# New ranks in a planned eight-layer transformer kernel, with an earlier start: what they do to the time

## The chip, the cores and the metric

The kernel runs on one core of one Trainium2 chip. The metric is device microseconds of one execution; the time before is the median of three runs. Engines are named as the profile names them: PE (TensorE matmul), PEld (TensorE weight load), DVE (VectorE), ACT (ScalarE), POOL (GpSimd) and SP (SyncE, which here only issues transfers).

## The reference

The input x has 8 sequences of 256 tokens of width 128, in fp32. Eight residual blocks follow one another, each with a layer norm ahead of it (`x = x + f(layernorm(x))`):

1. causal attention with one head: scores from `w_q` and `w_k` (width 64), softmax over the keys so far, values through `w_v1` and then `w_v2`;
2. a feed-forward block of width 512 with relu (only the first of eight experts counts, as the router's weights are set to one for it), with a layer norm of its own on input plus result;
3. attention without softmax, (theta phi^T) g over the sequence, so that it can be done as products of 128x128 matrices;
4. the same feed-forward block again;
5. retention with 16 heads: rotated queries and keys, a decaying causal mask, a norm for each head, a silu gate;
6. a feed-forward block of width 384, silu(gate) times up, with integer weights;
7. softmax attention with 16 heads of width 8, and low-rank additions to its weights;
8. the silu feed-forward block again.

Sequences are independent of each other through all of it.

## The kernel before

**Tiling.** The 8 sequences are 4 groups of two; a group's activations are one tile `x[g]` of 128 partitions by 4 token tiles by 128 columns. A matmul over a whole group gives a 128x512 result, one PSUM bank of fp32. There are 8 banks, and small pools of SBUF buffers (`work`, `small`, `probs`, `wide`, and others).

**Order.** Nothing in the code fixes the order of instructions by hand. While the program is built, a planner (`Plan`) runs all groups and layers as Python threads (generators). A thread yields what it needs next: `step(engine, us)`, an engine for an estimated time; `get(store)`, a buffer or a bank; `join`, other threads; `until`, a condition. The planner keeps a clock for each engine, goes through the steps in the order of its estimated times, and sends the thread on, which then issues its real instructions. Where several steps could start on an engine at once, the one of the thread with the lowest `rank` goes first (line 240), and after that the older one. Stores give out their items by rank too (`Store.next`). The order that results is written into each engine's queue and stays fixed; engines run their queues in that order and wait on semaphores. `HANDOFF`, `LOAD`, `NEW_MODE` and `LEEWAY` are costs that the planner adds to its estimates and no instructions.

**Ranks.** `plan.start(thread, rank, us)` starts a thread at a time. Before, group g runs all eight layers at rank g (`layers`), so group 0 always goes ahead of group 1, and so on. Preparing the weights (`causal_weights`, `linear_weights`, `retention_weights`, `silu_weights`, `softmax_weights`), filling the constant buffers (`constants`) and the very last feed-forward of each group have rank `LAST`, 4. The thread that forms the score matrices of the softmax attention, `pairs_of_scores`, has rank `FIRST`, -1.

**Start.** The inputs are loaded at the head of the program, x of group 0 in two halves. `causal_weights` multiplies the weights of the first layer with each other (lines 421 and 422) and copies the products from PSUM to SBUF (lines 424 and 425). `normalised` does a layer norm: for each tile, statistics on VectorE (lines 488 and 489), then four small operations for the whole group on GpSimd (lines 491 to 494: epsilon, sign, power, product), then the normalising on ScalarE or VectorE (lines 500 and 505). `transposed` transposes on TensorE (line 520) and copies to SBUF (line 393). `causal_attention` then waits for the products, and its first matmuls are the values (`by_tiles`, line 548) and the queries (line 561).

**Middle.** `ffn_relu` goes up at line 680 (activation at line 683) and down at line 693. `retention` has many matmuls on parts of the array (lines 816, 874, 896 and 904).

**Score stage.** In `softmax_attention_and_ffn` each sequence has 16 heads, taken two at a time: 8 items for the maxima (`firsts`) and 8 for the exponentials (`seconds`). `pairs_of_scores` puts one item (8 matmul instructions of line 1092, two banks) or two items side by side in the array's rows (16 instructions, four banks) on TensorE. After it come the maxima on VectorE (line 1113) or the exponentials on ScalarE (line 1147), and later the weighted sum (line 1164). Until the last group has been projected it holds four banks and waits to place two items at once. Then `todo["alone"]` is set, it takes two banks more, and two items go together only where two further banks are free at that moment; otherwise one goes by itself. The last feed-forward (lines 1006, 1012 and 1022) works on half a group at a time.

Of the kernel before, what the change touches and what calls it, by code (L numbers as in the profile page):

```python
# [33 lines left out]
P = 128  # L34
# [29 lines left out]
TABLE_LOAD = 1.3  # L64
NEW_MODE = 0.09
LOAD = 0.1
LEEWAY = 0.2


def of_act(n):  # L70
# [50 lines left out]
class Plan:  # L121
# [19 lines left out]
    def spawn(self, steps, rank=None):  # L141

        c = self.current
        th = Thread(steps, c.rank if rank is None else rank, c.t if c else 0.0, c.last if c else None)
        self.resume(th, None)
        return th
# [8 lines left out]
    def put(self, store, *items, later=0.0):  # L155
        for item in items:
            self.count += 1
            store.items.append((self.current.after() + later, self.count, item))
# [37 lines left out]
    def run(self):  # L196
        self.go = []
        while True:
            while self.go:
                self.resume(self.go.pop(0), None)  # L200
            fired = [u for u in self.untils if u[1]()]
            if fired:
                u = fired[0]
                self.untils.remove(u)
                u[0].t, u[0].last = max(u[0].after(), self.now), None
                self.resume(u[0], None)
                continue
            best = None
            if self.sleeping:
                best = (min(self.sleeping)[0], None, None)  # L210
            for e, queue in self.steps.items():
                if queue:
                    start = max(self.free[e], min(q[0] for q in queue))
                    if best is None or start < best[0]:
                        best = (start, e, None)
            for s in self.stores:
                found = s.next()
                if found and (best is None or found[0] < best[0]):
                    best = (found[0], None, s)
            if best is None:  # L220
                break
            start, e, s = best
            self.now = max(self.now, start)
            if e is None and s is None:
                nap = min(self.sleeping)
                self.sleeping.remove(nap)
                nap[2].t, nap[2].last = max(nap[2].t, start), None
                self.resume(nap[2], None)
                continue
            if s is not None:  # L230
                w = s.next()[1]
                s.waiting.remove(w)
                found = s.chosen(w[2])
                s.items = [i for i in s.items if not any(i is f for f in found)]
                got = [i[2] for i in found]
                w[0].t, w[0].last = start, None
                self.resume(w[0], got[0] if w[2] == 1 else got)
                continue
            able = [q for q in self.steps[e] if q[0] <= start]
            q = min(able, key=lambda q: (q[4] not in (None, self.table), q[1].rank, q[2]))  # L240
            _, th, _, us, table = q
            for queue in self.steps.values():
                queue[:] = [r for r in queue if r[1] is not th]
            if table not in (None, self.table):
                us += TABLE_LOAD
                self.table = table
            if e == PE:
                if th.mode != self.mode:
                    us += NEW_MODE
                elif q[0] > self.free[e] - LOAD:  # L250
                    us += LOAD
                self.mode = th.mode
            th.t, th.last = start + us, e
            self.free[e] = th.t
            self.resume(th, e)
        stuck = [s.waiting for s in self.stores if s.waiting] + self.untils
        assert not stuck, f"the plan is stuck at {self.now}: {stuck}"


def step(engine, us, table=None, mode=None):  # L260
    return ("step", ((engine, us, table),), mode)
# [6 lines left out]
def get(store, n=1):  # L268
    return ("get", store, n)


def join(threads):
    return ("join", list(threads))
# [11 lines left out]
def hybrid(ctx: ExitStack, tc: tile.TileContext, t: dict, out: bass.AP):  # L285
    nc = tc.nc
    plan = Plan()
    put, spawn = plan.put, plan.spawn
    FIRST, LAST = -1, GROUPS

    const = ctx.enter_context(tc.tile_pool(name="const", bufs=1))
    psum = ctx.enter_context(tc.tile_pool(name="psum", bufs=1, space=bass.MemoryType.PSUM))
# [66 lines left out]
    banks = [psum.tile([P, N], F32, tag=f"bank{i}", name=f"bank{i}") for i in range(8)]  # L359
    bank = plan.store(banks, strict=True)  # L360

    score_bank = plan.store([])
    work = buffers("work", 28, [P, WORK])
    small = buffers("small", 16, [P, P])
# [51 lines left out]
    def causal_weights():  # L416

        w = buffer("a_w", [P, 2, P])
        ps = yield get(bank)
        yield step(PE, 0.9)  # L420
        nc.tensor.matmul(ps[:, :P], a_t[:, 0, :], a_t[:, 1, :], start=True, stop=True)
        nc.tensor.matmul(ps[:, P : 2 * P], a_t[:, 2, :], a_v2, start=True, stop=True)
        yield step(DVE, 0.4)
        nc.vector.tensor_scalar_mul(w[:, 0, :], ps[:, :P], 0.125)
        nc.vector.tensor_copy(w[:, 1, :], ps[:, P : 2 * P])
        put(bank, ps)
        made["causal"] = w

    def linear_weights():

        w = buffer("b_w", [P, P])
        ps = yield get(bank)
        yield step(PE, 0.25)
        nc.tensor.matmul(ps[:, :P], b_tp[:, 1, :], b_tp[:, 0, :], start=True, stop=True)
        yield step(DVE, 0.2)
        nc.vector.tensor_scalar_mul(w, ps[:, :P], float(D**-0.5))
        put(bank, ps)
        made["linear"] = w
# [38 lines left out]
        made["softmax"] = w  # L477


    def layernorm(src, y):  # L480
        s = yield get(small)
        nt = src.shape[1]
        stats = view(s, "p (t c) -> p t c", 6 * nt, t=nt)
        mv = s[:, 24 : 24 + 2 * nt].rearrange("p (t c) -> p t c", t=nt)
        rstd, shift = s[:, 32 : 32 + nt], s[:, 36 : 36 + nt]
        for i in range(nt):
            yield step(DVE, 0.4)
            nc.vector.bn_stats(stats[:, i, :], src[:, i, :])  # L488
            nc.vector.bn_aggr(mv[:, i, :], stats[:, i, :])  # L489
        yield step(POOL, 1.14 + 0.16 * nt)  # L490
        nc.gpsimd.tensor_scalar(rstd, mv[:, :, 1], EPS, None, ALU.add)  # L491
        nc.gpsimd.tensor_scalar(shift, mv[:, :, 0], -1.0, None, ALU.mult)
        nc.gpsimd.tensor_tensor(rstd, rstd, minus_half[:, :nt], ALU.pow)  # L493
        nc.gpsimd.tensor_tensor(shift, shift, rstd, ALU.mult)  # L494

        def half(tiles):
            for i in tiles:
                e = yield either((ACT, 0.39), (DVE, 0.25))
                if e == ACT:
                    nc.scalar.activation(  # L500
                        y[:, i, :], src[:, i, :], AF.Identity, bias=shift[:, i : i + 1],
                        scale=rstd[:, i : i + 1],
                    )
                else:
                    nc.vector.tensor_scalar(
                        y[:, i, :], src[:, i, :], mv[:, i, 0:1], rstd[:, i : i + 1],
                        ALU.subtract, ALU.mult,
                    )

        yield join([spawn(half(range(k * nt // 2, (k + 1) * nt // 2))) for k in range(2)])  # L510
        put(small, s)
# [10 lines left out]
        put(bank, ps)  # L522
        return yT

    def normalised(g, keep=False, tiles=slice(0, NT)):
        y = yield get(work)
        nt = tiles.stop - tiles.start
        y4 = view(y, "p (t d) -> p t d", nt * D, t=nt)
        yield from layernorm(x[g][:, tiles, :], y4)
        yT = yield from transposed(y4)  # L530
        if keep:
            return y, y4, yT
        put(work, y)
        return yT
# [16 lines left out]


    def causal_attention(g):
        yT = yield from normalised(g)
        yield until(lambda: "causal" in made)
        w = made["causal"]

# [638 lines left out]
    def softmax_attention_and_ffn(g):  # L1196
# [15 lines left out]
        def sequence(b):  # L1212
# [51 lines left out]
            yield join([adding])  # L1264
            yield from add_to(g, tiles, ps[:, : 2 * D])
            put(bank, ps)
            yield join([spawn(ffn_silu(g, tiles), rank=LAST)])
            yield step(SP, 0.62)
            cols = slice(2 * b * D, 2 * (b + 1) * D)
            nc.sync.dma_start(out[g][:, cols], flat(x[g])[:, cols])  # L1270
# [4 lines left out]
        yield join([spawn(sequence(b)) for b in range(2)])  # L1275

    def layers(g):
        yield from causal_attention(g)
        yield from ffn_relu(g)
        yield from linear_attention(g)  # L1280
        yield from ffn_relu(g)
        yield from retention(g)
        yield from ffn_silu(g)
        yield from softmax_attention_and_ffn(g)

    plan.start(causal_weights(), LAST, 5.0)
    for g in range(GROUPS):
        plan.start(layers(g), g, 3.5 + 1.4 * g)
    plan.start(constants(), LAST, 8.0)
    plan.start(linear_weights(), LAST, 16.0)  # L1290
    plan.start(retention_weights(), LAST, 22.0)
    plan.start(silu_weights(), LAST, 24.0)
    plan.start(softmax_weights(), LAST, 24.0)
    plan.start(pairs_of_scores(), FIRST, 0.0)
    plan.run()
    return plan
# [108 lines left out]
```

## Time and profile before

| | |
|---|---|
| time before, median of 3 | 478.56 us (478.03 to 479.53) |
| span of the profiled execution | 474.9 us |
| mean granted TensorE clock | 0.982 |
| instructions | 13095 |
| HBM read, written | 4.56 MB, 1.05 MB |

The profile is of one execution and somewhat shorter than the timed runs. Part 1 of the page gives each engine's busy time as a share of the span. In part 2 each digit is a fortieth of the span (11.9 us), in tenths; the row PEclk is the clock that TensorE was granted. The view of stretches gives busy microseconds and, in brackets, instructions in each stretch of time. In the timeline an entry is start, duration, engine, line, operation, and operands with shapes; the square brackets hold the engine's idle time before it and what ended it. The chain is the work that ended last, followed back from the last instruction.

### The profile page before, as it was taken

The numbers are of one execution on the slowest core, as the hardware profiler recorded it, in microseconds if no ns is written. First come the engines' busy times: TensorE is split into PE (matmuls) and PEld (weight loads), VectorE is DVE, ScalarE is ACT, GpSimd is POOL, SyncE is SP. The second block draws the span as 40 slices with busy tenths as digits, with TensorE's granted clock in tenths as the row PEclk, the third lists the DMA queues.
The fourth block names the chain that finished last, engine by engine and source line by source line (L and its number), as shares of the span: only waits on it lengthen the run. The fifth ranks groups of instructions, "written<-read, shape, count | busy, mean of one in ns | idle before, by whom it ended". The sixth has DMA issues, their size and how long they took to land.

```text
span 474.9 us, 13095 instructions
## 1 busy us (share of the span) xinstructions
PE 437.3 (92%) x5340; PEld 303.3 (64%) x5340; DVE 341.0 (72%) x975; ACT 254.7 (54%) x505; POOL 133.1 (28%) x245
## 2 busy tenths in 40 slices
PE   3989989879979997999999999998899999899996
PEld 1767775837667575756676557665567676566565
DVE  6699777779839894899667957774858674595223
ACT  4787536354330534154556385633659857436862
POOL 6106867494702563133211111311002012010011
PEclk9999999989989999999999999998979999999999
DMA  8200000001100300301000031010010001100000
GB/s 275 109 2 0 3 1 0 1 0 31 17 4 1 48 2 4 59 11 24 3 12 20 1 48 24 4 26 4 2 25 13 11 16 24 36 3 13 2 12 23
DMA packets 8044, 10.90 MB, mean 23 GB/s; under 512 B 1000, under 2 KB 6888, under 8 KB 7984
## 3 DMA queue, kind: packets, MB, share of 16 engines
q1 hardware_dynamic: 7904, 9.94, 9.2%
q8 instruction: 42, 0.69, 0.6%
q14 instruction: 18, 0.15, 0.1%
q10 hardware_dynamic: 80, 0.13, 0.1%
HBM read 4.56 MB, written 1.05 MB: 12 GB/s over the span
## 4 chain that ended last, share of the span: by engine, by line
PE 68%; DVE 13%; POOL 4%; issue 4%; ACT 3%; ACTq 0%; DVEq 0%; POOLq 0%
PE bank L1092 16%; PE bank L1164 6%; PE bank L1006 4%; PE bank L693 4%; PE bank L680 4%; PE bank L1022 4%; PE bank L1012 4%; PE bank L874 3%; DVE small L1113 3%; PE bank L749 2%; PE bank L816 2%; PE bank L904 2%; PE bank L959 2%; PE bank L520 2%; PE bank L1177 2%
## 5 line engine op out<-in xcount | busy, mean ns | idle before, releaser
L1113 DVE TENSOR_REDUCE small<-bank 128x2 f32<-128x512 f32 x128 | 80.8, 681 | 29.5 <-PE bank L1092 29.3
L1147 ACT ACTIVATE probs<-bank 128x512 f32<-128x512 f32 x128 | 68.1, 598 | 42.4 <-PE bank L1092 41.9
L1092 PE MATMUL bank<-l_spread 32*128 32x256 f32 x1024 | 89.3, 409 | 0.5 <-ACT probs L1147 0.3
L491 POOL TENSOR_SCALAR small<-small 128x4 f32<-128x4 f32 (+1 forms) x44 | 11.2, 254 | 238.3 <-DVE small L489 214.2
L1092 PEld LDWEIGHTS bank<-l_spread 32*128 32x128 f32 x1024 | 55.7, 188 | 24.9 <-issue 14.7
L393 ACT COPY work<-bank 128x512 f32<-128x512 f32 (+3 forms) x79 | 36.8, 476 | 63.7 <-PE bank L1164 14.8
L500 ACT ACTIVATE work<-x,small 128x128 f32<-128x128 f32 x79 | 34.0, 485 | 28.9 <-POOL small L494 28.7
L493 POOL TENSOR_TENSOR small<-small,mhalf 128x4 f32<-128x4 f32 (+1 forms) x44 | 43.4, 987 | 0.0
L488 DVE BATCH_NORM_STATS2 small<-x 128x6 f32<-128x128 f32 x128 | 34.5, 269 | 4.0 <-DMA x<-in_x 3.6
L680 PE MATMUL bank<-work,c_relu 128*128 128x512 f32 x64 | 31.7, 632 | 3.1 <-ACT work L393 3.0
L1164 PE MATMUL bank<-probs,l_values 128*32 128x256 f32 x512 | 32.0, 388 | 1.7 <-ACT work L1008 1.7
L489 DVE BATCH_NORM_AGGREGATE small<-small 128x2 f32<-128x6 f32 x160 | 29.1, 182 | 5.5
L693 PE MATMUL bank<-c_relu,work 128*128 128x128 f32 x256 | 31.8, 276 | 0.1
L683 ACT ACTIVATE work<-bank,c_relu 128x512 f32<-128x512 f32 x30 | 20.6, 686 | 21.0 <-PE bank L680 21.0
L693 PEld LDWEIGHTS bank<-c_relu,work 128*128 128x128 f32 x256 | 30.4, 192 | 1.7 <-issue 1.4
L393 DVE COPY work<-bank 128x512 f32<-128x512 f32 (+3 forms) x33 | 18.5, 564 | 17.2 <-PE bank L520 4.9
L520 PE MATMUL bank<-ident,work 128*128 128x128 f32 x128 | 23.3, 294 | 6.9 <-ACT work L500 5.8
L1006 PE MATMUL bank<-work,c_ints 128*128 128x256 f32 (+1 forms) x72 | 26.2, 479 | 2.4 <-ACT work L393 2.4
L1022 PEld LDWEIGHTS bank<-c_ints,work 128*128 128x128 f32 x192 | 23.3, 191 | 4.7 <-issue 3.0
L1022 PE MATMUL bank<-c_ints,work 128*128 128x128 f32 x192 | 25.9, 282 | 0.1
L520 PEld LDWEIGHTS bank<-ident,work 128*128 128x128 f32 x128 | 15.1, 145 | 16.2 <-ACT work L500 9.6
L1012 PE MATMUL bank<-work,c_ints 128*128 128x256 f32 (+1 forms) x72 | 25.2, 460 | 0.1
(147 smaller groups left out, 787.2 us busy)
## 6 DMA issues: line engine op xcount, KB each, us to landing
r_spread<-wide SPq DMA_DIRECT2D x32, 64.0 KB
l_spread<-wide SPq DMA_DIRECT2D x32, 64.0 KB
out<-x SPq DMA_DIRECT2D x8, 128.0 KB
c_retention_qk<-in_retention_qk SPq DMA_DIRECT2D x1, 770.0 KB
x<-in_x SPq DMA_DIRECT2D x3, 256.0 KB
c_retention_vo<-in_retention_vo SPq DMA_DIRECT2D x1, 713.0 KB
c_relu<-in_relu SPq DMA_DIRECT2D x1, 706.0 KB
c_ints<-in_ints SPq DMA_DIRECT2D x1, 576.0 KB
```

The costliest lines, as they stand in the source:

```text
L393: (nc.scalar.copy if e == ACT else nc.vector.tensor_copy)(dst, src)
L493: nc.gpsimd.tensor_tensor(rstd, rstd, minus_half[:, :nt], ALU.pow)
L520: nc.tensor.transpose(ps[:, i * P : (i + 1) * P], y[:, i, :], ident)
L680: nc.tensor.matmul(ps, w1[:, c * P : (c + 1) * P], yT[:, :N], start=True, stop=True)
L693: nc.tensor.matmul(ps[:, n * D : (n + 1) * D], h[c][:, i * P : (i + 1) * P], w2[:, c, :], start=(c == 0), stop=(c == 3),)
L1006: nc.tensor.matmul(ps[:, :n], w_gate[:, cols], yT[:, :n], start=True, stop=True)
L1012: nc.tensor.matmul(ps[:, :n], w_up[:, cols], yT[:, :n], start=True, stop=True)
L1022: nc.tensor.matmul(ps[:, (i - first) * D : (i - first + 1) * D], h[c][:, i * P : (i + 1) * P], w_down[:, c, :], start=(c == 0), stop=(c == 2),
L1092: nc.tensor.matmul(to[k][:, n * S : (n + 1) * S], seq.spread[rows, j, of_keys, n * P : (n + 1) * P], seq.spread[rows, j, 1 - of_keys, :], ...
L1113: nc.vector.tensor_reduce(nmax[:, h2 % 4 // 2, 2 * (h2 % 2) + k, :], ps[k].rearrange("p (m s) -> p m s", m=2), AX.X, ALU.max, negate=True,)
L1147: nc.scalar.activation(p[:, k, :], ps[k], AF.Exp)
L1164: nc.tensor.matmul(o[32 * i : 32 * (i + 1), (j % 2) * S : (j % 2 + 1) * S], seq.v[:, c, VONE * h : VONE * h + 32], seq.p[h2][0][:, k, c * ...
```

## The change

The change does four things.

- **Ranks by layer.** `RANKS[g]` gives each group a rank for each of its first seven layers (the eighth entry is for the last feed-forward), so that, for example, group 3's softmax attention goes before group 2's. `FIRST` becomes -3.5 and `LAST` 11.78. On TensorE a step that would become ready only just before it starts (within `LOAD`, 0.1 us) has 1.95 added to its rank (`LATE`), so that a step which has been ready for longer goes first. `LEEWAY` goes from 0.2 to 0.29, and the start times of groups and weight threads are new.
- **First layer norm.** The layer norm ahead of the causal attention has its first two small operations (epsilon and sign) on VectorE instead of GpSimd, in all groups (`quick`), and group 0 does it in two halves of two tiles, each with its own statistics, powers and normalising. The transposes follow when both halves are done.
- **The weights' products at once.** `causal_weights` runs at rank `FIRST` from 3.8 us, so that its copies aren't behind the groups' work.
- **Ten identity products.** Six products of the identity with itself are put on TensorE at the very start, and four after the weights' products; nothing reads them. They are to keep TensorE busy.

```diff
 LOAD = 0.1
-LEEWAY = 0.2
+ARRIVALS = (3.1, 5.1, 6.8, 8.3)
+LEEWAY = 0.29
+RANKS = [
+    [-0.43, -1.33, -1.23, -2.16, 0.4, -1.26, 1.32, 4.87],
+    [-0.32, 1.61, 0.5, 1.51, -0.96, -0.46, -1.85, 1.67],
+    [2.33, 2.23, 2.97, 7.68, 2.15, -1.02, 3.92, 2.82],
+    [3.09, 3.56, 6.8, 10.82, 2.27, 3.76, -2.79, 2.52],
+]
+FIRST, LAST = -3.5, 11.78
+LATE = 1.95
...
-            q = min(able, key=lambda q: (q[4] not in (None, self.table), q[1].rank, q[2]))
+
+            late = {id(q): e == PE and q[0] > start - LOAD for q in able}
+            q = min(
+                able, key=lambda q: (q[4] not in (None, self.table), q[1].rank + LATE * late[id(q)], q[2])
+            )
...
-    FIRST, LAST = -1, GROUPS
...
+    def keep_busy(ps, n):
+
+        for _ in range(n):
+            nc.tensor.matmul(ps[:, :P], ident, ident, start=True, stop=True)
+
+    keep_busy(banks[0], 6)
...
-        ps = yield get(bank)
-        yield step(PE, 0.9)
+        ps, idle = yield get(bank, 2)
+        yield step(PE, 2.0)
         nc.tensor.matmul(ps[:, :P], a_t[:, 0, :], a_t[:, 1, :], start=True, stop=True)
         nc.tensor.matmul(ps[:, P : 2 * P], a_t[:, 2, :], a_v2, start=True, stop=True)
+        keep_busy(idle, 4)
+        put(bank, idle)
...
-        yield step(POOL, 1.14 + 0.16 * nt)
-        nc.gpsimd.tensor_scalar(rstd, mv[:, :, 1], EPS, None, ALU.add)
-        nc.gpsimd.tensor_scalar(shift, mv[:, :, 0], -1.0, None, ALU.mult)
+        if quick:
+            yield step(DVE, 0.13)
+        else:
+            yield step(POOL, 1.14 + 0.16 * nt)
+        e = nc.vector if quick else nc.gpsimd
+        e.tensor_scalar(rstd, mv[:, :, 1], EPS, None, ALU.add)
+        e.tensor_scalar(shift, mv[:, :, 0], -1.0, None, ALU.mult)
+        if quick:
+            yield step(POOL, 0.66 + 0.16 * nt)
...
-        yield from layernorm(x[g][:, tiles, :], y4)
+        parts = 2 if quick and g == 0 else 1
+        yield join(
+            [
+                spawn(layernorm(a, b, quick))
+                for a, b in zip(halved(x[g][:, tiles, :], parts), halved(y4, parts))
+            ]
+        )
...
-        yT = yield from normalised(g)
+        yT = yield from normalised(g, quick=True)
...
-            yield join([spawn(ffn_silu(g, tiles), rank=LAST)])
+            yield join([spawn(ffn_silu(g, tiles), rank=RANKS[g][7])])
...
-        yield from causal_attention(g)
-        yield from ffn_relu(g)
-        yield from linear_attention(g)
-        yield from ffn_relu(g)
-        yield from retention(g)
-        yield from ffn_silu(g)
-        yield from softmax_attention_and_ffn(g)
-
-    plan.start(causal_weights(), LAST, 5.0)
+        for layer, rank in zip(
+            (
+                causal_attention, ffn_relu, linear_attention, ffn_relu, retention, ffn_silu,
+                softmax_attention_and_ffn,
+            ),
+            RANKS[g],
+        ):
+            plan.current.rank = rank
+            yield from layer(g)
+
+    plan.start(causal_weights(), FIRST, 3.8)
     for g in range(GROUPS):
-        plan.start(layers(g), g, 3.5 + 1.4 * g)
-    plan.start(constants(), LAST, 8.0)
-    plan.start(linear_weights(), LAST, 16.0)
-    plan.start(retention_weights(), LAST, 22.0)
-    plan.start(silu_weights(), LAST, 24.0)
-    plan.start(softmax_weights(), LAST, 24.0)
+        plan.start(layers(g), g, ARRIVALS[g])
+    plan.start(constants(), LAST, 29.7)
+    plan.start(linear_weights(), LAST, 8.6)
+    plan.start(retention_weights(), LAST, 27.1)
+    plan.start(silu_weights(), LAST, 22)
+    plan.start(softmax_weights(), LAST, 57.7)
     plan.start(pairs_of_scores(), FIRST, 0.0)
```

More of the change, by code (lines that the diff above doesn't have):

```diff
@@ L477, in softmax_weights, with layernorm @@
         made["softmax"] = w
-    def layernorm(src, y):
+    def layernorm(src, y, quick=False):
         s = yield get(small)
@@ L523, in transposed, with halved, normalised @@
         return yT
-    def normalised(g, keep=False, tiles=slice(0, NT)):
+    def halved(a, parts):
+        n = a.shape[1] // parts
+        return [a[:, k * n : (k + 1) * n] for k in range(parts)]
+    def normalised(g, keep=False, tiles=slice(0, NT), quick=False):
         y = yield get(work)
```

## The prediction

> **What bounds the kernel now.** I read the page's busy shares first, then the stretches of time, the timeline of the start, and last the chain that ended last.
>
> ```profile
> PE 437.3 (92%) x5340; PEld 303.3 (64%) x5340; DVE 341.0 (72%) x975; ACT 254.7 (54%) x505; POOL 133.1 (28%) x245
> ...
> PEclk9999999989989999999999999998979999999999
> ```
>
> TensorE (PE) is the bound over the whole. Only 474.9 - 437.3 = 37.6 us of it is idle, so new ranks can gain only from that, from a lower clock, or from PE work that costs more than it need. I make a ledger of these losses. The granted clock averages 0.982: (1 - 0.982) x 474.9 = 8.5 us, in the dips of the PEclk row. Now the stretches (start:end, then busy us and count of PE, PEld, DVE, ACT, POOL, then clock, DMA share and GB/s):
>
> ```profile
> 0.00:12.00 12.00, 3.88 (x12) 2.26 (x12) 7.89 (x39) 4.96 (x10) 7.62 (x29) 1.00 0.82 277
> 12.00:24.00 12.00, 11.69 (x55) 9.31 (x56) 7.53 (x22) 9.02 (x15) 1.51 (x4) 1.00 0.26 103
> 24.00:36.00 12.00, 10.65 (x67) 8.18 (x67) 11.55 (x37) 10.77 (x33) 0.00 (x0) 1.00 0.01 2
> 36.00:48.00 12.00, 10.89 (x73) 8.51 (x72) 11.38 (x53) 8.46 (x22) 7.88 (x14) 1.00 0.00 0
> ...
> 456.00:475.00 19.00, 14.85 (x108) 11.31 (x106) 7.29 (x23) 6.61 (x15) 2.64 (x8) 1.00 0.07 22
> ```
>
> Of the idle time, 12.0 - 3.88 = 8.1 us lies in the first 12 us and 19.0 - 14.85 = 4.2 us in the last stretch, a serial tail (last feed-forward, then the output transfer). Some 25 us lie between. From 24 to 48 us VectorE is 96% busy, so an earlier start helps only because VectorE itself idles 4.5 us between 12 and 24. The timeline of the start says why:
>
> ```profile
> 6.91 1.65 ACT L500 ACTIVATE work<-x,small 128x128 f32<-128x128 f32 x4 [2.40 <-POOL small L494]
> ...
> 9.88 0.68 DVE L393 COPY work<-bank 128x512 f32<-128x512 f32 x1
> ...
> 11.98 0.28 DVE L425 COPY a_w<-bank 128x128 f32<-128x128 f32 x1
> ...
> 12.31 2.07 PE L548 MATMUL bank<-a_w,work 128*128 128x128 f32 x8 [1.50 <-DVE a_w L425]
> ...
> 22.93 1.16 PE L548 MATMUL bank<-a_w,work 128*128 128x128 f32 x8
> ```
>
> The transposed activations of group 0 are there at 10.56 (9.88 + 0.68), but the weights' products, finished on PE at 5.1, leave PSUM only at 12.26, behind all four groups' statistics: their thread has the lowest rank. And the same eight matmuls take 2.07 us at 12.31 and 1.16 at 22.93: PE runs at half speed until about 18.4, when the spacing of matmuls falls from 0.21 to 0.11 us. That half-speed stretch of 6.1 us loses 3.0 us.
>
> The chain that ended last gives the other end of the ledger (start, us, what):
>
> ```profile
> 408.38 1.08 PE bank L1092 x16
> 410.04 1.06 PE bank L1092 x8
> 411.73 1.06 PE bank L1092 x8
> 413.43 1.06 PE bank L1092 x8
> ```
>
> L1092 makes score matrices. Sixteen matmuls, two items side by side, take 1.08 us; eight, one item alone, take 1.06. From 408 to 457 us, with the last group alone, I count 20 single items and 6 pairs, and PE is busy 48.9 of 49 us. Pairing those 20 would save 20 x 1.06 - 10 x 1.08 = 10.4 us of PE. Earlier there are only 8 singles.
>
> [...] the granted clock shows 1.00 for 0 to 12 us nevertheless, so there I trust the durations. [...]
>
> **The change part by part.** *Ten identity products.* Six are put on PE first, once the identity is there (written at about 1.35 us). Each fp32 product is two PE instructions here (four tiles of L548 are eight), cold 0.21 us each: 6 x 2 x 0.21 = 2.6 us, from about 1.5 to 4.1. The queue behind them on PE is only the weights' products, which need a transfer that lands at 3.88: a delay of 0.2 us, hidden since nothing wants them before 9 us. Then the products (0.9 us cold), then four more: 4 x 2 x 0.21 = 1.7 us, to 6.7. Nothing waits behind them, as group 0's transposes start later. So they cost nothing, and PE is busy for 5.2 us on end. Gain: between nothing [...] and the full 3.0 us; I take 2.0.
>
> *First layer norm in halves, two small operations moved to VectorE, products copied at once.* Before: statistics of four tiles end at 4.93, GpSimd takes 5.02 to 6.87, normalising and transposes run to 9.12, the copy to 10.56, the weights to 12.26. After: the second half decides. Its statistics end at 4.93 again; two small VectorE operations at about 0.15 (the 128x2 reciprocal's duration) give 5.25; the power waits for the first half's GpSimd work and then takes 0.71 and 0.20 (the two-column forms near the end of the trace) with gaps, to about 6.4; normalising two tiles, 0.6 to 0.9, to 7.2; four transposes, 0.9 cold, to 8.1; copy 0.7 and handoffs: queries near 9.0. That is 12.3 - 9.0 = 3.3 us sooner. The copies of the weights (2 x 0.28) go into VectorE's stream at about 5.2 and push later statistics back by 0.6. Each other group loses about 0.5 us on GpSimd (its two operations there, 0.25 and 0.24) and adds 0.3 on VectorE. Since VectorE binds again from 24 us, I count 2.5 of the 3.3. Start together: -4.5 us, bounds -1.5 and -6.3.
>
> *Start times of weights.* The fills of `constants` (7 x 0.6 + 8 x 1.0 = 12 us on ScalarE at 12 to 28) move behind 29.7; ScalarE is idle 24.7 us between 50 and 100 (25.34 busy of 50), before retention needs them at about 103. The softmax weights (0.54 + 0.23 of VectorE) leave the stretch where VectorE is full. Cost nothing, hidden by that idle time.
>
> *Ranks by layer, LATE, LEEWAY.* These add no instruction; they reorder. Group 2's and 3's second relu layers get ranks 7.68 and 10.82, so they wait until little else is ready and become filler for the softmax stage; the last group's softmax gets -2.79, above all other work. What can this touch? PE waits on ACT, DVE or POOL with no other group ready: 7.1 us in 62 to 105, 1.2 at 272, 2.6 in 338 to 347, 1.7 at 405 (the idle times of PE's rows in the timeline), together 12.6. Two clock dips follow such idling: 0.93 over 96 to 120 us and 0.86 over 336 to 360, so 24 x (0.07 + 0.14) = 5.0 us lost. The single items in the tail, 10.4. Sum 28 us. Not touched: four stalls with no releaser ahead of L874 and L904 (2.0 + 1.4 + 1.1 + 1.7 us), and the tail after 457. Moving an idle place is easier than removing it, and the score stage has its own floor: an item costs VectorE 2 x 0.68 or ScalarE 2 x 0.60, so 32 items in sequence need 16 x 1.36 + 16 x 1.20 = 41 us even when paired, against 49. A quarter of the 28 is what I take: -7.5 us, bounds +8 (below) and -16.
>
> Sum: -4.5 - 7.5 = -12.0; 478.56 - 12.0 = 466.5 us.
>
> **The rivals.**
> 1. *Only the start gains* and the reorder is a wash: 478.6 - 4.5 = 474. For it: from 200 to 300 PE is busy 97.8 of 100 us, where no order can help. Against: the holes at 62 to 105 and 338 to 405 are exactly cases of no other group ready.
> 2. *The reorder gives over half of its 28 us*, with filler saved for the score stage: 478.6 - 5 - 16 = 457.5. For it: the holes, dips and singles are all after-effects of too little independent work at hand. Against: the 41 us floor.
> 3. *Slower.* The `alone` switch is thrown when the last group is projected, whatever the others still have to do. With group 3 at rank -2.79 it may be thrown while another group's items are open: then two of eight banks are left for all other work and items go singly. If 24 more items go singly, that is 24 x 0.52 = 12.5 us, and with the start's gain 478.6 - 4.5 + 12.5 = 486.6. For it: 20 of 32 items go singly in that mode now. Against: the held-back relu layers and group 3's own chain come first, so group 3 should still be last.
>
> **How the numbers follow.** Forecast 0.50, rival 1 0.22, rival 2 0.13, rival 3 0.11, and 0.04 for start and reorder cancelling to no change. Faster by over 0.3% (below 477.1): 0.50 + 0.22 + 0.13 = 0.85, less 0.02 for the forecasts' own spread: 0.83. Same 0.05, slower 0.12. The range takes in rivals 1 and 2 and a small loss: 456 to 479, leaving out some 0.1 above and less below.
>
> **What would show it.** Right: the first L561 near 9 to 10 us at about half its former length; L425 before 6 us; L683 appearing after 200 us; fewer x8 pieces of L1092 in the last 60 us; PE idle below 30 us. Wrong: L1092 in eights well before the last stretch, a wait before retention on `constants`, VectorE over 96% beyond 48 us, or a mean clock below 0.98.

## The result and the profile after

The changed kernel takes 459.63 us (457.73 to 460.03), the kernel before 479.04 on the same chip: a ratio of 0.9578, 95% interval 0.9529 to 0.9627. That is 19.4 us less, where 12.0 was forecast, and inside the range. The direction held. Much of the working behind the number did not, as the experiments show. Ratios, here and below, compare only executions within 1.5% of the fastest of their kernel while medians are over all, and the profiles of late_zero and flat_ranks fell outside that, so no span or clock is read from those two.

The page of the changed kernel, busy time and granted clock:

```profile
PE 436.2 (95%) x5360; PEld 306.1 (67%) x5360; DVE 338.9 (74%) x979; ACT 236.7 (52%) x497; POOL 132.3 (29%) x239
...
PEclk9999899999999999995989999999999999999999
```

The span fell by 17.1 us, from 474.9 to 457.8. TensorE's busy time fell by 1.1 and its idle time by 16.0, from 37.6 to 21.6. But 5.0 us of what was idle is now filled by the identity products, whose results nothing reads. The kernel without them (no_identity, below) splits its gain into 14.9 us less idle time and 8.0 us less busy time. So most of the gain is idle time, and not all of it. Two other entries of the ledger stayed put: the clock is 0.981, a loss of 0.019 x 457.8 = 8.7 us (8.5 before), though the dips are at other places (the digit 5 lies at about 206 to 217 us); and 24 score items still go singly. An item of the ledger that I had not kept is ScalarE: its busy time fell by 18.0 us. The kernel before loads an activation table 28 times at 1.28 us, the changed one 14 times, which is those 18 us.

The stretches, in the form shown before:

```profile
0.00:12.00 12.00, 8.66 (x34) 7.58 (x35) 8.05 (x46) 3.73 (x6) 5.88 (x20) 1.00 0.81 282
12.00:24.00 12.00, 11.24 (x64) 8.80 (x63) 8.47 (x27) 6.87 (x21) 1.21 (x2) 1.00 0.25 100
24.00:36.00 12.00, 12.00 (x69) 8.60 (x68) 11.44 (x45) 8.94 (x25) 6.61 (x13) 1.00 0.00 0
36.00:48.00 12.00, 12.00 (x83) 9.98 (x82) 9.85 (x35) 12.00 (x20) 5.59 (x9) 1.00 0.01 2
439.00:458.00 19.00, 14.95 (x90) 12.50 (x89) 8.83 (x27) 6.77 (x15) 2.64 (x8) 1.00 0.07 22
```

In the first 12 us PE is busy 4.8 us more than before, but the identity products alone are 5.0. The tail is as long as it was. What is really fuller is 24 to 100 us. Before (first line, of the kernel before) and after:

```profile
24.00:100.00 76.00, 66.29 (x415) 50.56 (x414) 63.01 (x230) 44.65 (x106) 43.70 (x73) 1.00 0.00 1
```

```profile
24.00:100.00 76.00, 73.53 (x428) 54.25 (x427) 65.90 (x236) 50.91 (x109) 51.02 (x85) 0.98 0.00 1
```

The timeline of the start, after:

```profile
6.70 0.28 DVE L448 COPY a_w<-bank 128x128 f32<-128x128 f32 x1
...
8.39 0.59 ACT L414 COPY work<-bank 128x512 f32<-128x512 f32 x1 [1.07 <-PE bank L549]
...
10.28 0.79 PE L457 MATMUL bank<-c_linear 32*128 32x128 f32 x2 [1.93 <-DMA c_linear<-in_linear]
...
11.00 2.08 PE L587 MATMUL bank<-a_w,work 128*128 128x128 f32 x8
12.87 1.92 PE L600 MATMUL bank<-work,a_w 128*128 128x512 f32 x2
```

The transposed activations are there at 8.98 (8.39 + 0.59), as I had said. The weights' products leave PSUM by 6.98 (6.70 + 0.28), later than the 6 us that I had named as a sign, but early enough. But the values (L587) start at 11.00 and the queries (L600) at 12.87, both at half rate: 2.08 and 1.92 us, where the same lines take 1.05 at 17.11 and 1.02 at 18.00. In PE's queue the product of the *linear* attention's weights (L457) stands ahead of them, and PE does it first: it waits 1.93 us for `c_linear`, from 8.4 to 10.3, while the values' inputs have been there since 8.98. Its thread's start time went from 16.0 to 8.6 us in the change.

### The profile page after: what moved, and what is told of

The parts are those of the page before. It is cut to its first block, busy times and chain, and to the rows that moved or that the text cites. A ratio compares the mean times of both kernels' runs of the same rounds, so it can differ in the third digit from the quotient of the medians.

```text
span 457.8 us, 13125 instructions
## 1 busy us (share of the span) xinstructions
PE 436.2 (95%) x5360; PEld 306.1 (67%) x5360; DVE 338.9 (74%) x979; ACT 236.7 (52%) x497; POOL 132.3 (29%) x239
## 3 DMA queue, kind: packets, MB, share of 16 engines
HBM read 4.56 MB, written 1.05 MB: 12 GB/s over the span
## 4 chain that ended last, share of the span: by engine, by line
PE 74%; DVE 12%; ACT 5%; issue 3%; POOL 2%; DMA 1%; SPq 1%; DVEq 0%
PE bank L1131 17%; PE bank L1203 7%; PE bank L1061 5%; PE bank L1045 5%; PE bank L1051 4%; PE bank L855 4%; PE bank L719 3%; PE bank L732 3%; PE bank L587 3%; PE bank L549 2%; PE bank L890 2%; PE bank L788 2%; PE bank L913 2%; DVE small L511 2%; DVE small L1152 2%
## 5 line engine op out<-in xcount | busy, mean ns | idle before, releaser
L1131 PE MATMUL bank<-l_spread 32*128 32x256 f32 x1024 | 89.3, 409 | 2.3 <-issue 2.3
L1131 PEld LDWEIGHTS bank<-l_spread 32*128 32x128 f32 x1024 | 56.1, 188 | 26.3 <-issue 12.0
L518 POOL TENSOR_SCALAR small<-small 128x4 f32<-128x4 f32 (+1 forms) x40 | 10.0, 250 | 216.2 <-DVE small L512 201.2
L414 ACT COPY work<-bank 128x512 f32<-128x512 f32 (+3 forms) x86 | 40.2, 484 | 53.5 <-PE bank L549 14.3
L529 ACT ACTIVATE work<-x,small 128x128 f32<-128x128 f32 x80 | 34.7, 485 | 37.8 <-POOL small L523 37.6
L1203 PE MATMUL bank<-probs,l_values 128*32 128x256 f32 x512 | 34.0, 390 | 0.5 <-DVE work L1225 0.5
L582 DVE TENSOR_TENSOR x<-bank,x 128x256 f32<-128x256 f32 (+1 forms) x36 | 15.9, 448 | 13.2 <-PE bank L587 4.2
L1045 PE MATMUL bank<-work,c_ints 128*128 128x256 f32 (+1 forms) x72 | 24.8, 462 | 0.5 <-ACT work L414 0.5
L1203 PEld LDWEIGHTS bank<-probs,l_values 128*32 128x32 f32 x512 | 13.9, 111 | 16.7 <-issue 6.1
L414 DVE COPY work<-bank 128x512 f32<-128x512 f32 (+3 forms) x26 | 13.7, 535 | 15.2 <-PE bank L1203 6.6
L1061 PE MATMUL bank<-c_ints,work 128*128 128x128 f32 x192 | 24.6, 279 | 0.1
L1051 PE MATMUL bank<-work,c_ints 128*128 128x256 f32 (+1 forms) x72 | 24.0, 456 | 0.0
```

The source lines that it names most:

```text
L414: (nc.scalar.copy if e == ACT else nc.vector.tensor_copy)(dst, src)
L1045: nc.tensor.matmul(ps[:, :n], w_gate[:, cols], yT[:, :n], start=True, stop=True)
L1051: nc.tensor.matmul(ps[:, :n], w_up[:, cols], yT[:, :n], start=True, stop=True)
L1061: nc.tensor.matmul(ps[:, (i - first) * D : (i - first + 1) * D], h[c][:, i * P : (i + 1) * P], w_down[:, c, :], start=(c == 0), stop=(c == 2),
L1131: nc.tensor.matmul(to[k][:, n * S : (n + 1) * S], seq.spread[rows, j, of_keys, n * P : (n + 1) * P], seq.spread[rows, j, 1 - of_keys, :], ...
L1203: nc.tensor.matmul(o[32 * i : 32 * (i + 1), (j % 2) * S : (j % 2 + 1) * S], seq.v[:, c, VONE * h : VONE * h + 32], seq.p[h2][0][:, k, c * ...
```

## The experiments

Ratios are to the kernel before on the same chip. Lines shift from kernel to kernel: the score line is L1092 before, L1131 in the changed kernel, L1129 without identity products. "Full-clock" is span times granted clock, a rough measure. Single items are counted in the timeline of the score line, with the low clock allowed for; two items side by side that stall midway look like two single ones, so a count can be off by two to four.

| kernel | us | ratio (95%) | span | clock | full-clock | PE idle | singles |
|---|---|---|---|---|---|---|---|
| before | 479.04 | 1 | 474.9 | 0.982 | 466.4 | 37.6 | 24 |
| changed | 459.63 | 0.958 (0.953 to 0.963) | 457.8 | 0.981 | 449.1 | 21.6 | 24 |
| start_only | 486.41 | 1.017 (1.009 to 1.025) | 485.2 | 0.961 | 466.3 | 29.6 | 34 |
| ranks_only | 467.83 | 0.983 (0.973 to 0.992) | 465.2 | 1.000 | 465.2 | 32.4 | 34 |
| ranks_copies | 478.75 | 1.004 (1.001 to 1.008) | 477.2 | 0.964 | 460.0 | 31.5 | 32 |
| late_zero | 471.93 | 0.987 (0.979 to 0.994) | | | | | |
| flat_ranks | 479.70 | 0.999 (0.995 to 1.003) | | | | | |
| rounded | 506.09 | 1.058 (1.053 to 1.063) | 506.1 | 0.949 | 480.3 | 47.7 | 36 |
| no_held_relu | 466.27 | 0.977 (0.972 to 0.982) | 465.3 | 0.981 | 456.5 | 23.9 | 34 |
| last_softmax | 465.05 | 0.976 (0.970 to 0.981) | 461.1 | 0.980 | 451.9 | 27.9 | 26 |
| no_identity | 453.76 | 0.949 (0.944 to 0.955) | 452.1 | 0.992 | 448.5 | 22.7 | 24 |
| identity_first | 456.59 | 0.953 (0.946 to 0.960) | 456.4 | 0.978 | 446.4 | 23.3 | 26 |
| linear_first | 450.97 | 0.947 (0.943 to 0.951) | 449.0 | 0.996 | 447.2 | 22.5 | 24 |
| linear_first_id | 453.67 | 0.952 (0.948 to 0.956) | 451.0 | 0.996 | 449.2 | 23.3 | 24 |

**The two halves of the change.** `start_only` keeps the start's edits and puts back ranks, FIRST, LAST, LATE, LEEWAY and weight times:

```diff
-LEEWAY = 0.29
+LEEWAY = 0.2
-RANKS = [ ... ]
-FIRST, LAST = -3.5, 11.78
-LATE = 1.95
+RANKS = [[g] * 7 + [4] for g in range(4)]
+FIRST, LAST = -1, 4
+LATE = 0
...
-    plan.start(constants(), LAST, 29.7)
-    plan.start(linear_weights(), LAST, 8.6)
+    plan.start(constants(), LAST, 8.0)
+    plan.start(linear_weights(), LAST, 16.0)
...
```

> The start's edits alone: new arrival times, first layer norm in halves and on VectorE, weights' products at once, ten identity products; the ranks, LATE, LEEWAY and weight start times of before. Theory A (the two parts add: start some 5 us, order some 14): 474 us, PE idle down by about 5 us, all of it in the first 24 us. Rival B (the order of the rest brings it all, the start's gain is eaten by VectorE being full from 24 to 48 us): 477 to 480. Rival C (the gain belongs to the combination; any other plan falls at random): anywhere from 470 to 490, unrelated to the start.

It is 1.7% slower than before, which only C's range (470 to 490) takes in. Its PE idle time did fall by 8 us, and in the first 100 us PE is busy 91.1 us against 81.9 (5.0 of the difference are the identity products). But the planner laid the rest out anew: ten more single items, and the clock at 0.961.

`ranks_only` is the converse: the start as it was, all else new (causal weights at `LAST`, no halves, no identity products).

> The new ranks, LATE, LEEWAY and weight start times alone, with the start as before. Theory A: 465 us, and the first matmul of the queries at 12 us as before. Rival B: 460. Rival C: the ranks were set with the new start and don't fit the old one, so 470 or more.

467.8 us, between A's 465 and C's 470. But its full-clock span is 465.2, like that of before (466.4): by this measure, what this kernel gains is that in the profiled execution the clock hardly dips (1.00 up to 438 us, 0.98 after it). Neither half shortens the full-clock span by more than 1.2 us; together they take 17.3. The parts don't add, which speaks for C. PE's idle time comes nearer to adding: 8.0 and 5.2 us less alone, 16.0 together. What each half loses again is busy time, with 34 single items instead of 24.

`ranks_copies` adds to it the early copy of the weights' products:

```diff
-    plan.start(causal_weights(), LAST, 5.0)
+    plan.start(causal_weights(), FIRST, 3.8)
```

> The new ranks, LATE, LEEWAY and weight start times, and of the start's edits only that the weights' products are copied at once; group 0's layer norm whole and on GpSimd, arrival times of before, no identity products. With the ranks alone the span was 465.2 us, with all but the identity products 452.1. Theory A (what the ranks need is an early first attention, and the copies are what held it back): about 456, PE idle over the first 24 us below 8 us, and 24 to 100 us filled as in the changed kernel (PE busy 72 or more of 76). Rival B (the halved layer norm on VectorE does it): still about 465. Rival C (any other plan falls at random): off both by more than 5 us, with the difference spread over the whole span.

10 to 11 us slower than without the edit, although PE has 4.2 us more of busy time in the first 100 us (84.7 against 80.5). A falls, and B with it. C's number comes out, but the difference isn't spread over the span. The loss is clock: 0.036 x 477.2 = 17.2 us, above all one dip in the single items of the end (0.72 over 400 to 438 us):

```profile
400.00:438.00 38.00, 36.63 (x223) 22.13 (x224) 22.62 (x45) 15.82 (x30) 2.67 (x8) 0.72 0.03 4
```

PE is busy 96% of that stretch, and its clock is 0.72 all the same. In the changed kernel, 12 of the 18 pieces of score work that start between 400 and 435 us are single items too, and the clock over 400 to 438 is 1.00 with PE busy 37.0 us; so single items alone don't account for the dip. Its cause is not shown.

**LATE and the 32 ranks.** `late_zero`:

```diff
-LATE = 1.95
+LATE = 0
```

> The changed kernel with LATE = 0, so that a TensorE step which has just become ready is no longer put behind older ones. Theory A (steps issued the moment their input is ready leave PE short gaps): 462 to 464, PE idle up by 3 to 5 us in many short gaps. Rival B (LATE only reshuffles): within 2 us of 459.6 either way. Rival C: 465 or more, in a few large gaps.

12 to 14 us more than with it: C's number. Where they go can't be read from its profile.

`flat_ranks` starts from the changed kernel without identity products and puts the ranks back to the group's number:

```diff
-RANKS = [ ... ]
+RANKS = [[g] * 7 + [4] for g in range(4)]
```

> The changed kernel without identity products, with the 32 ranks put back to the group's number (4 for the last feed-forward); FIRST, LAST, LATE, LEEWAY and start times stay new. Theory A (ranks by layer keep filler for PE): 464 to 470 us, with the lost time as PE idle between 24 and 200 us, as in the kernel before. Rival B (LATE and the start do it, the 32 numbers add little): within 3 us of 453.8. Rival C (chance of the plan): 475 or more, as with the start alone (486.4).

No better than the kernel before, which is C's number, so the 32 numbers are worth 5% there (0.999 against 0.949), some 24 us. A also named the wrong stretch. The traces show PE executing the same sequence as in no_identity up to 100 us, and just as full:

```profile
24.00:100.00 76.00, 73.55 (x430) 54.31 (x429) 65.73 (x236) 50.80 (x109) 50.48 (x85) 0.98 0.00 1
```

So the early filling needs neither the ranks by layer nor LATE (late_zero: 73.0 of 76), each taken out alone. It comes with what is left: the start, the new weight times, FIRST, LAST and LEEWAY, which no run separates further. The start's edits alone don't bring it (start_only 69.7), nor does the rest without them (ranks_only 67.3). By itself it saves no time at the end: with the old ranks all of it is given back, and not before 200 us (from 100 to 200 PE is busy 97.6 us, in no_identity 98.7).

`rounded` keeps the pattern of the ranks and rounds each to a half (-0.43 to -0.5, 7.68 to 7.5, and so on).

> The changed kernel without identity products, with the 32 ranks rounded to halves, so that the pattern stays (who is held back, who goes ahead) and the exact numbers go. Theory A (the pattern does it): within 4 us of 453.8. Rival C (the exact order was picked among many, and any neighbour is worse): 460 or more, and the loss in other places than before.

506 us, 52 more than with the exact numbers, and slower than any other kernel here. Two ranks that differed (-0.43 and -0.32) are now equal; the sequence on PE parts at 21 us, and from there everything moves: 25 us more idle, 12 more single items, and a clock that dips in nine of the forty slices (0.051 x 506.1 = 25.8 us lost, against 0.008 x 452.1 = 3.6).

```profile
PEclk9999999999999888999999789999989699968999
```

This is the clearest result. My theory, that the *pattern* of the ranks (filler held back, the last group ahead) makes the gain, falls as an account of its size. The gain belongs to this particular order more than to its pattern.

Two single entries of the pattern, each changed in the kernel without identity products. `no_held_relu`:

```diff
-    [2.33, 2.23, 2.97, 7.68, 2.15, -1.02, 3.92, 2.82],
-    [3.09, 3.56, 6.8, 10.82, 2.27, 3.76, -2.79, 2.52],
+    [2.33, 2.23, 2.97, 2.97, 2.15, -1.02, 3.92, 2.82],
+    [3.09, 3.56, 6.8, 6.8, 2.27, 3.76, -2.79, 2.52],
```

> The changed kernel without identity products, with two of the 32 ranks changed: the second relu layer of group 2 at 2.97 instead of 7.68, of group 3 at 6.8 instead of 10.82. Theory A (these layers are held back as filler for the score stage): 458 to 462, with the relu lines ended before 170 us and PE idle up after 200. Rival C (the place of these layers matters little; the exact order does): either within 3 us of 453.8, or over 465 through low clock, without more idle time of PE in the score stage.

Some 13 us slower, which is C's number, and not as A has it. The relu activations end at 190 us, and with the high ranks at 180. Of the 256 matmuls of the way down (line 730), 24 come after the first score matmul (at 195 us), and with the high ranks 16 (at 187). So the high ranks kept hardly anything back for the score stage. Idle time differs by 1.2 us. Ten more single items (10 x 0.53 = 5.3 us) and a clock of 0.981 against 0.992 (5.2 us) make most of the difference.

`last_softmax` is one number, -2.79 to 4.0 for group 3's softmax attention.

> The changed kernel without identity products, with one of the 32 ranks changed: group 3's softmax attention at 4.0 instead of -2.79, behind the other groups' instead of ahead of nearly all. The order differs late only. Theory A (going ahead lets the last group's chain, which sets the end, run early): 457 to 460, with the last score matmul later than 429 us. Rival (the last group has the engines to itself by then): within 1 us of 453.8.

11 to 13 us slower, more than A's 457 to 460; the last score matmul comes at 433 instead of 429. Here A's mechanism shows in part. The last group's two closing layers run with nothing to fill their gaps: 5.1 of the 9.0 us by which the span is longer are idle time of PE. The clock is lower as well: 0.84 after 438 us, and L1043 takes 2.93 us for six, where the same six take 1.56 in the changed kernel (L1045, at 444.89):

```profile
444.03 0.69 PE L547 MATMUL bank<-ident,work 128*128 128x128 f32 x2 [2.88 <-ACT work L527]
445.18 2.93 PE L1043 MATMUL bank<-work,c_ints 128*128 128x256 f32 x6 [0.46 <-ACT work L413]
```

**The identity products.** `no_identity` keeps the plan and the order, and leaves out the ten:

```diff
-    keep_busy(banks[0], 6)
...
-        keep_busy(idle, 4)
```

> The changed kernel, same plan and order, without the ten identity products. Theory A, corrected by the trace after (the products run cold from 1.4 to 7.5 us and the matmuls at 11 us are cold all the same): within 1 us of 459.6, with the full clock from about 16 us as with them. Rival (they do bring the full clock forward, from 18.4 to 16 us): 461 to 462, half-rate matmuls to 18 us or later.

453.76 us (453.04 to 453.78): 5.9 us faster than with them by the medians, 4.0 by the ratios, which neither theory had. At the start they bring nothing: values at 11.00 with and 10.54 without, PE busy 73.5 us at a clock of 0.98 from 24 to 100 us in both, and by 92 us the two run level (idle time ahead of the same relu matmul begins at 92.3 and 92.5). They part after 200 us: the same score matmuls start 0.8 us apart at 206 (206.28 and 205.48) and 4.9 us apart at 225 (224.84 and 219.99). The same stretch, with the products and without:

```profile
204.00:249.00 45.00, 41.20 (x835) 27.41 (x824) 34.99 (x92) 22.17 (x50) 11.38 (x18) 0.85 0.04 9
```

```profile
204.00:249.00 45.00, 42.39 (x861) 28.52 (x861) 37.80 (x100) 25.72 (x56) 10.58 (x17) 1.00 0.04 10
```

0.15 x 45 = 6.8 us of clock lost in one and not in the other, while both have the same 1.5 us of idle time at 204 to 206. The other executions lean the same way: clock 0.977 to 0.989 in four with the products, 0.988 to 0.992 in four without. But clock is not all of it, as the one at 0.989 took 457.73 us and the one at 0.988 without the products 453.74. PE's stalls without a releaser, in which it waits for nothing that the profile shows, differ too. With them:

```profile
PE bank L913 <- issue: 3.8, 2, 2.1
PE bank L1131 <- issue: 2.3, 1, 2.3
```

and without:

```profile
PE bank L911 <- issue: 2.9, 2, 2.3
```

`identity_first` keeps the first six only.

> The changed kernel with six identity products at the start and not the four after the weights' products; same plan and order. Theory A (they don't bring the full clock forward; the 6 us between 453.8 without and 459.6 with ten come later, from low-clock windows and instruction stalls that move with them): somewhere from 453 to 460, full clock from about 16 us, and the difference to 453.8 explained by (1 - clock) x span and stalls without a releaser. Rival (each product costs its own time on the path): 453.8 + 6/10 x 5.9 = 457.3, with the first matmul of the values later than at 10.5 us.

456.59 us, between the two. Both numbers of the rival come out (457.3, and values later than 10.5, at 11.20), so the time alone doesn't refute a price for each product. The profile speaks against it: the values wait for `c_linear` and not for products, and the full-clock span (446.4) is no longer than without any (448.5); clock (0.978) and stalls moved again. The timeline of its start shows the weights' products at full rate behind the six (0.59 and 0.38 us, where the kernel before takes 0.79 and 0.63). Full rate is lost again at 7.9 us, ahead of the wait for `c_linear`, which begins at 8.4, and so not through it; PE had been idle 1.38 us from 5.1. From 7.9 to 14.8 the granted clock is 0.50, and the values take 2.08:

```profile
4.28 0.59 PE L442 MATMUL bank<-c_causal 64*128 64x128 f32 x2
4.71 0.38 PE L443 MATMUL bank<-c_causal 64*128 64x128 f32 x2
6.48 0.78 PE L548 MATMUL bank<-ident,work 128*128 128x128 f32 x2 [1.38 <-ACT work L528]
...
10.48 0.79 PE L456 MATMUL bank<-c_linear 32*128 32x128 f32 x2 [2.04 <-DMA c_linear<-in_linear]
11.20 2.08 PE L586 MATMUL bank<-a_w,work 128*128 128x128 f32 x8
```

`linear_first` takes the wait for `c_linear` away by issuing the smaller transfer first, without identity products and with plan and order unchanged; `linear_first_id` does the same with them.

```diff
-    w1, w2, b1, b2, gamma, beta = load("relu")
     b_tp, b_g = load("linear")
+    w1, w2, b1, b2, gamma, beta = load("relu")
```

> The changed kernel without identity products, with the transfer of c_linear issued ahead of that of c_relu; plan and TensorE order unchanged. In the runs so far TensorE's queue has the product of the linear attention's weights ahead of group 0's values, and waits for c_linear from 8.3 to 9.8 us. Theory A (that wait is on the path): values start at about 9.2 instead of 10.5 us, and 1 to 1.5 us go from the end: 452.5. Rival (VectorE, full from 24 to 48 us, takes the gain back): 453.8, with the gain seen at 12 us and gone at 50.

> The changed kernel with its ten identity products, and c_linear issued ahead of c_relu. Six products released the clock from 4.5 to 7.9 us in one run[...]. Theory A (with that idle time gone the released clock lasts): first values and queries at full rate (four tiles in about 1.1 us instead of 2.1), 2 us less than the same kernel without the products. Rival (the products bring nothing here either): half-rate until 14 us, and at or above the time without them, up to 459.

Without the products: values at 9.74 instead of 10.54, and 450.97 us, the lowest time here. By the ratios that is 1.2 us less than no_identity, well inside both intervals, so the time doesn't settle it. In the profiles the span is 3.1 us shorter, 1.8 of it clock, and the first score matmul still comes 2.0 us earlier (185.3 against 187.3), so VectorE didn't take the gain back. With them, what they are for does happen in the profiled execution:

```profile
9.19 0.48 PE L457 MATMUL bank<-c_linear 32*128 32x128 f32 x2 [0.65 <-DMA c_linear<-in_linear]
9.60 1.16 PE L587 MATMUL bank<-a_w,work 128*128 128x128 f32 x8
```

The values take 1.16 us instead of 2.08, the matmuls of the start stay at full rate from 4.5 us on (L600 takes 1.02 us at 10.60, 1.91 in linear_first), and this kernel is 1.5 to 1.9 us ahead of linear_first from 15 to 90 us. That the transfer makes the difference is not shown: in the changed kernel, with the same ten products, PE was at half rate until about 16.0 us, so there was no full rate that the wait could have cost. Then PE stalls 2.0 us at 116 us within L913 with no releaser, and at the first score matmul the lead is gone (185.6 against 185.3). The span ends 2.0 us later (453.67 us), nearly all of it lost after 280 us; this kernel's clock is 0.99 from 200 to 400 us and 0.98 after 438, and linear_first's is 1.00 in these stretches. By the ratios the two aren't apart. So Theory A has the start right and the end wrong, and a gain of the start lasts only until something later takes it.

## Why the prediction was right, and where it was not

- **PE is the bound, and idle time is what can be won: right in the main.** 16.0 of 17.1 us of the span, though 5.0 of them are only filled with identity products; without those, 14.9 of 22.8.
- **Clock and single items as things to recover: wrong.** I counted on a quarter of 28 us with 5.0 from clock and 10.4 from singles. Neither moved: 8.5 to 8.7 us, 24 to 24 items. I had also read two pairs of items at half clock, at 327 and 349 us (2.02 us each, against 1.08), as four singles.
- **Identity products "cost nothing", gain 2.0: wrong.** That keeping PE busy at the head brings full rate sooner was my estimate; no trace of the kernel before shows it. With them the kernel takes 4 to 6 us longer, and 2 to 3 where `c_linear` comes first, which the intervals don't separate. The immediate part of the step was right (they lie beside nothing that PE is wanted for), and the gain at the start exists, but of the five kernels that have all ten or the first six, one shows it (linear_first_id). That the clock would differ late in the run as well (0.85 with them and 1.00 without over 204 to 249 us) was not in my bounds of 0 to 3.0.
- **Queries near 9.0: wrong.** The 9.0 was set against 12.31, which is the start of the values; they start at 11.00 and the queries at 12.87. It failed through a step that I filed under "cost nothing": the new start time of the linear weights. I looked at what engines do and not at the order in one queue, where a product without urgency waits for a transfer ahead of urgent work.
- **Start -4.5 and order -7.5, added: wrong as a sum.** Alone they measure +1.7% and -1.7%, together -4.2%. The term that was mis-sized is the reorder; its bounds, -16 to +8, hold the sum only because they were wide. They are too narrow for what a reorder can do: rounding alone moves it by 52 us.
- **Held-back relu layers as filler for the score stage: wrong** (their activations end at 180 us, score matmuls begin at 188, and 16 of 256 matmuls of the way down come after that). **Last group's softmax ahead: right in part** (last_softmax: 5.1 of its 9.0 us there are idle time, most of the rest is clock).
- **Of the signs named ahead**, PE idle below 30 us came true. First queries at 9 to 10 at half their length, the copy of the weights' products before 6 us, relu activations after 200 us and fewer lone items did not.

So the forecast's direction held because the profile showed idle time that an order could fill; its mechanism is confirmed for the idle time and, in part, for the last group alone. That it held for this order is in good part luck: the same terms, less the 2.0 of the identity products, would have given `rounded`, with the same pattern, 10 us, and it is 5.8% slower than the kernel before. Why this order fits so much better than its neighbours stays open. The halved number of table loads (28 to 14) goes along with it, but rounded has 20 and is the slowest, and no run isolated them.

## What to carry to other kernels

Where a planner with priorities writes the order, a change of a priority is a new program: price it as a draw with a spread (here 454 to 506 us from changes to the 32 ranks alone, in five kernels), not as a sum of terms, and measure neighbours before explaining the winner. Take parts of a bundle out one at a time on the same order: the two best steps here were to remove one (no identity products) and to issue a small transfer ahead of a large one, 453.76 and 450.97 us, the second not clear of the noise. And follow each engine's queue for work that isn't urgent and waits ahead of work that is (1.93 us in the changed kernel).

## What the hardware did that I had not expected

TensorE's clock dips in stretches where PE is busy almost throughout: 0.72 over 38 us with PE busy 96% (ranks_copies), 0.85 over 45 us with 92% (changed kernel). The longest gap in that stretch of the changed kernel is 2.3 us, and the one ahead of the dip at 207 is 1.5 us:

```profile
206.08 0.28 PE L1165 MATMUL bank<-ident,small 128*16 128x128 f32 x1 [1.47 <-DVE small L1152]
206.28 1.33 PE L1131 MATMUL bank<-l_spread 32*128 32x256 f32 x16
207.54 1.28 PE L890 MATMUL bank<-r_values,work 64*128 64x272 f32 x4
208.75 1.11 PE L549 MATMUL bank<-ident,work 128*128 128x128 f32 x4
```

```profile
207.10:217.40 10.30, 10.30 (x40) 4.61 (x32) 6.97 (x15) 3.06 (x5) 2.79 (x3) 0.50 0.01 2
```

In no_identity the same gap comes before the same work, which runs at full rate (0.73 us where the changed kernel takes 1.28, and 0.66 where it takes 1.11):

```profile
205.28 0.28 PE L1163 MATMUL bank<-ident,small 128*16 128x128 f32 x1 [1.47 <-DVE small L1150]
205.48 1.15 PE L1129 MATMUL bank<-l_spread 32*128 32x256 f32 x16
206.56 0.73 PE L888 MATMUL bank<-r_values,work 64*128 64x272 f32 x4
207.22 0.66 PE L547 MATMUL bank<-ident,work 128*128 128x128 f32 x4
```

So the length of this gap alone doesn't decide. What does is not shown: there is one profile of each kernel, and whether the products have a part in the dip at 207 stays open.

Behind six identity products, from 1.4 to 4.3 us, PE is at full rate from about 4.5 in two kernels (identity_first, linear_first_id: the second of the weights' products takes 0.38 us). The changed kernel begins with the same six, and there it takes 0.63. PE works from 1.4 to 8.4 us without a gap in its timeline, and the transposes at the end of that still run at half rate (1.06 us for four, against 0.60 at 18.86). Full rate first comes at about 16.0 us. What makes the difference is not shown.

PE's stalls with no releaser, 0.7 to 2.3 us in these timelines, differ in size and place between the kernels with and without the twenty PE instructions at the head: 1.71 us within L913 at 119 us with them, none in the same matmuls (L911 at 118 us) without. Their cause is not shown.
